# A Chebyshev graph convolution block on one core: the dense work of a block two groups later, its aggregate placed ready transposed, node numbers written to PSUM, the first own rows loaded whole, unread products ahead of the look-ups

## The chip, the cores and the metric

The kernel runs on one core of a Trainium2 chip. Its engines are TensorE (PE; PEld is its weight load), VectorE (DVE), ScalarE (ACT), GpSimd (POOL) and SyncE (SP), which here only issues DMAs. The metric is the device time in microseconds (us); the time before is 2028.2 us, the median of three runs (2027.43 to 2034.34).

## The reference

`x` has N = 6250 rows of D = 512 floats; `src` and `dst` have E = 100000 entries, sorted by `dst`. Cut to what matters:

```python
h = maximum(layernorm(x), 0)
deg = segment_sum(ones(E), src);  dinv = where(deg > 0, 1 / sqrt(max(deg, 1)), 0)
norm = -dinv[src] * dinv[dst]
conv = lambda h, W0, W1, b: h @ W0 + segment_sum(h[src] * norm[:, None], dst) @ W1 + b
h = layer_norm(conv(h, W1_0, W1_1, b1)) * gamma + beta
h = where(h >= 0, h, 0.01 * h)
out = x + conv(h, W2_0, W2_1, b2)
```

So each of the two layers gathers 100000 rows of 2 KB by index, adds them into 6250 nodes, and multiplies the nodes' own rows and the sums by a 512x512 matrix each. All is 32-bit floating point.

## The kernel before

**First phase** (before `usual_path`). x is read in tiles of 128 nodes, and its mean and variance are taken. The degrees are counted by one-hot matmuls in bf16 (lines 417 and 440). The table of the first layer, `tab[0]`, gets 528 numbers a row: 512 of relu(layernorm(x)) times dinv (L340) and dinv itself (L478). Meanwhile POOL already gathers the first 76 chunks of 128 edges out of raw `x` (L291); their normalization is made up for later.

**Chunks, units, groups, blocks.** The edges are cut into 782 chunks of 128. One indirect DMA (L548), issued by POOL, fetches the 128 rows of a chunk into a slot of a ring in SBUF (`places`; the first twelve chunks sit in tiles that later hold weights and biases, `lent`). Three chunks are a unit, which adds into 32 columns of nodes; four units are a group of 12 chunks and 128 columns. Group 0 has only one unit, and there are 66 groups in a layer, so group g holds the chunks from 12g - 9 to 12g + 2. A block is 128 nodes; there are 49, and a block's nodes lie in two or three groups.

**Work of a group.** `choose` on DVE writes the numbers of the nodes that a column stands for (`node`, L678, 128x128) and compares them with the edges' destinations to a 0/1 matrix `sel` (L689, 128x384). In layer 0, for chunks from 76 on, `scale` (L729) multiplies `sel` by the dinv that came with each gathered row. `sums` (L745) then multiplies the 12 gathered chunks by `sel` on PE, with 12 matmuls of 128x512 into `ps`, and ACT copies the sums to SBUF (`agg`, L760). The first 76 chunks hold raw x: for them PE looks up scale and shift of each edge by matmuls (`look_up` L598 with L601, L604 and L607 on DVE, `find` L583 and L586), and ACT applies them in place (L609, a Relu per chunk).

**Work of a block.** `place` (L781) adds the rows of the block's two or three groups into `an_ps` by 0/1 matrices `there` (L768, DVE); ACT scales the result by -dinv (L880); PE turns it (four transposes, L888) and DVE copies that to `aT` (L890). The node's own rows `h` come back from the table by eight DMAs (`load_h`, L622: 32 rows apart in a fashion that lets DVE's 32x32 transposes, L632, finish the turn). PE multiplies both: own rows by one matrix (L648, four matmuls of 128x512), aggregate by the other (L643, four more, into the same PSUM sum). `finish` adds the bias, normalizes and writes the row to the second layer's table (L849 to L866), or adds x and writes the output (L843 to L846). The last four blocks' own rows are done ahead (`early`).

**What sets the order.** The order of PE, POOL and SP is written out by hand in `usual_path`: what the program says is the order of the queue. DVE's and ACT's order is the scheduler's, which is held by `issue_after` at some places. In the order before, block work of a group's end comes around that group's `sums`: for groups 3 to 5 of layer 0 behind them, else ahead of them, and the second product (L643) one step later (`left`).

**The ring.** `ring` (L46) says which chunk sits in which slot and which chunk had it before, and `gather_to` lets POOL issue only those gathers whose slot was read by a `sums` that has already been written down. POOL's queue is in order, so a gather whose slot is not yet read holds all later ones. Before, the ring has 55 slots, and from a hundred or so chunks on it shrinks slowly, lap by lap: to 35 in the first layer and to 26 in the second.

Of the kernel before, what the change touches and what calls it, by code (L numbers as in the profile page):

```python
# [26 lines left out]
Q = 32  # L27
NQ = P // Q
STEP = 3
DRIFT = 32  # L30
RE = 14
# [8 lines left out]
NARROW = 26  # L40

# [6 lines left out]
def ring(chunks, lent, most, full):  # L48
# [25 lines left out]
def gnn_kernel(  # L74
# [54 lines left out]
    def dup(ap, n):  # L129
# [16 lines left out]
    ndeg = const.tile([P, NB], F32, name="ndeg")  # L146
# [31 lines left out]
    nodes_ps = stay.enter_context(tc.tile_pool(name="nodes_ps", bufs=1, space=bass.MemoryType.PSUM)).tile(  # L178
        [P, D], F32, name="nodes_ps")
    assert NQ * NS + 1 <= D - P  # L180
# [169 lines left out]
    def turn_dst(wps):  # L350
# [17 lines left out]
        first_ps = nodes_ps[:, : NQ * NS + 1]  # L368
# [78 lines left out]
    with tc.tile_pool(name="fold", bufs=1) as dp, tc.tile_pool(  # L447
# [15 lines left out]
        nc.vector.tensor_mul(ndeg, ndinv, dinv)  # L463

    for i0, n in others:
# [9 lines left out]
        nc.vector.tensor_copy(places[:, RE + i0 : RE + i0 + n, D : D + 1], dinv[:, cols, None])  # L475
        make_table(i0, n)
    early = NB - LAST
# [13 lines left out]
def usual_path(tc, have):  # L491
    nc = tc.nc
    (x, out, tab, root, ndeg, ndinv, sidx, dlx, iota_r, w_sb, W2_1, W2_0, w_late, ident, eps, ones, first, nodes_ps, node_of, minus,
     unsorted, dinv, sdinv, bias1, bias2, gam, bet, unseen, unit, N, E, D, NB, NC, NU, NS, KD, rows, places, R,
     load_rest, sc, pick, quads, src_hi, zero_row, p_id, lent, X, src, W) = (
        have[n] for n in ("x out tab root ndeg ndinv sidx dlx iota_r w_sb W2_1 W2_0 w_late ident eps ones first nodes_ps node_of "
                          "minus unsorted dinv sdinv bias1 bias2 gam bet unseen unit N E D NB NC NU NS KD rows places "
                          "R load_rest sc pick quads src_hi zero_row p_id lent X src W").split())
    AHEAD = 2
    SOON = range(3, 6)  # L500
# [10 lines left out]
    with ExitStack() as es:  # L511
# [12 lines left out]
        own_row, begun = {}, set()  # L524
# [9 lines left out]
        slots, prev = ring(NC, X, R + LATER, R)  # L534
# [54 lines left out]
        def look_up(tag):  # L589
# [7 lines left out]
            for j in range(4):  # L597
# [5 lines left out]
            both = pool.tile([P, D], F32, name="an")[:, : 8 * NB].rearrange("p (j k b) -> p j k b", j=4, k=2)  # L603
            nc.vector.tensor_tensor(both, at_lo[:, :, : 2 * NB].rearrange("p j (k b) -> p j k b", k=2),  # L604
                                    is_hi[:, :, None, :].to_broadcast([P, 4, 2, NB]), op=OP.mult)
# [19 lines left out]
        def load(layer, i):  # L625
            if i not in EARLY:
                load_h(layer, i, pool.tile([P, D], F32, name="h", bufs=AHEAD))
# [819 lines left out]
```

## Time and profile before

| | us |
|---|---|
| median of three runs | 2028.2 |
| the profiled execution | 2038.83 |
| its span | 2037.0 |
| PE busy | 1637.0 (80%) |
| DVE busy | 745.5 (37%) |
| ACT busy | 332.8 (16%) |
| POOL busy | 1494.5 (73%) |
| gathers of L548 out of the tables (`sidx` 1191, `lidx` 270) | 1134.0 + 256.1 |

The profile page names an engine's busy time, then groups of equal instructions: line, engine, operation, output<-input, shape, count, then busy time, mean duration of one in ns, idle time just ahead of them and who ended it. The windows view gives, for each stretch of the span, each engine's busy time with the number of its instructions in brackets, then TensorE's granted clock, the share of the DMA engines and GB/s. The timeline has a row for each instruction or run of equal ones: start, duration, engine, line, operation, tiles, count, and in brackets how long the engine had waited and for whom. A busy engine is not the same as the bound: PE is busy 80% of the span, and POOL 73%, but POOL's time has an issue gap behind each gather.

### The profile page before, as it was taken

Reading aid. Unit: us, or ns where it says so; the run is one execution under the profiler, and the core shown is the slowest. Engines: PE = TensorE matmul, PEld = TensorE weight load, DVE = VectorE, ACT = ScalarE, POOL = GpSimd, SP = SyncE. Lnnn points to the kernel's source line nnn. Section 1 sums busy time; section 2 is a strip of 40 time slices with the busy share of each in tenths; the row PEclk is TensorE's granted clock in tenths of the full one; section 3 lists DMA queues with packets and bytes.
Section 4 is the critical chain, followed back from the end, with each engine's and each line's share of the span. In section 5 each row is a group of like instructions: output and inputs, shape, how many; then the busy total and the mean of one; then the engine's idle time right before and its main releaser. Section 6 shows DMA issues by size and latency. Waiting matters only on the chain.

```text
span 2037.0 us, 18838 instructions
## 1 busy us (share of the span) xinstructions
PE 1637.0 (80%) x6458; PEld 626.0 (31%) x6458; DVE 745.5 (37%) x1554; ACT 332.8 (16%) x605; POOL 1494.5 (73%) x1578
## 2 busy tenths in 40 slices
PE   5478997678787677878888887888888878888888
PEld 4443342223232222333233222223222222223333
DVE  8965554243453333543453221222222222222221
ACT  8775111011110110111110000000000000000000
POOL 4576677777777777777777777777777777777775
PEclk9779998889888889888899899999998899989999
DMA  9998788888888888888887888888888888888885
GB/s 340 392 328 250 231 249 241 243 237 247 253 255 243 237 242 241 251 245 253 248 235 234 254 249 252 241 256 245 246 253 249 244 253 255 237 254 261 261 245 174
DMA packets 225518, 515.56 MB, mean 253 GB/s; under 512 B 38796, under 2 KB 90570, under 8 KB 225414
## 3 DMA queue, kind: packets, MB, share of 16 engines
q0 software_dynamic: 125120, 415.88, 68.7%
q1 hardware_dynamic: 100253, 98.38, 15.1%
q8 instruction: 53, 0.87, 0.2%
q14 instruction: 52, 0.42, 0.1%
q10 hardware_dynamic: 40, 0.02, 0.0%
HBM read 475.25 MB, written 38.86 MB: 252 GB/s over the span
## 4 chain that ended last, share of the span: by engine, by line
POOL 42%; PE 18%; issue 18%; DMA 14%; DVE 7%; ACT 1%; SPq 0%; DVEq 0%; POOLq 0%; ACTq 0%
POOL places L548 42%; DMA places<-tab,sidx 9%; PE ps L745 5%; PE u_ps L643 4%; PE u_ps L648 4%; DMA places<-tab,lidx 3%; PE an_ps L781 2%; DVE hi L417 1%; DVE lo L417 1%; DMA w<-in_L_gnn_W_dram 1%; DVE st L852 1%; PE hT_ps L888 1%; DVE u_ps L849 1%; PE hT_ps L598 1%; DMA h<-tab 1%
## 5 line engine op out<-in xcount | busy, mean ns | idle before, releaser
L548 POOL DMA_INDIRECT places<-tab,sidx x1191 | 1134.0, 952 | 378.0 <-issue 336.1
L745 PE MATMUL ps<-places,sel 128*32 128x512 f32 x3104 | 522.0, 667 | 169.2 <-DMA places<-tab,sidx 96.2
L781 PE MATMUL an_ps<-agg,there 128*128 128x512 f32 (+1 forms) x554 | 277.0, 634 | 109.4 <-ACT agg L760 109.4
L548 POOL DMA_INDIRECT places<-tab,lidx x270 | 256.1, 948 | 82.3 <-issue 78.1
L745 PEld LDWEIGHTS ps<-places,sel 128*32 128x32 f32 x3104 | 102.3, 117 | 555.5 <-DMA places<-tab,sidx 205.1
L689 DVE TENSOR_TENSOR sel<-dlx,nodes_ps 128x384 f32<-128x384 f32 (+3 forms) x134 | 72.4, 541 | 445.5 <-PE ps L745 432.9
L648 PE MATMUL u_ps<-w,hT 128*128 128x512 f32 x392 | 182.0, 608 | 25.4 <-DVE hT L632 22.5
L781 PEld LDWEIGHTS an_ps<-agg,there 128*128 128x128 f32 (+1 forms) x554 | 108.1, 201 | 263.6 <-issue 141.7
L760 ACT ACTIVATE agg<-ps 128x512 f32<-128x512 f32 (+2 forms) x130 | 76.2, 588 | 639.8 <-PE ps L745 612.2
L648 PE MATMUL u_ps<-places,hT 128*128 128x512 f32 x392 | 177.8, 597 | 0.0
L643 PE MATMUL u_ps<-w,aT 128*128 128x512 f32 x384 | 173.3, 594 | 2.3 <-DVE aT L890 2.3
L643 PE MATMUL u_ps<-places,aT 128*128 128x512 f32 x384 | 173.4, 593 | 0.8 <-DVE aT L890 0.8
L729 DVE TENSOR_TENSOR sel<-sel,places 128x384 f32<-128x384 f32 (+9 forms) x76 | 35.3, 466 | 368.6 <-DMA places<-tab,sidx 363.9
L855 ACT ACTIVATE sd<-mv,eps 128x1 f32<-128x1 f32 (+1 forms) x49 | 14.4, 295 | 600.4 <-DVE mv L853 600.3
L632 DVE STREAM_TRANSPOSE hT<-h 128x512 f32<-128x512 f32 x90 | 63.6, 707 | 129.0 <-PE u_ps L648 120.6
L648 PEld LDWEIGHTS u_ps<-w,hT 128*128 128x128 f32 x392 | 72.7, 196 | 102.5 <-issue 76.5
L643 PEld LDWEIGHTS u_ps<-w,aT 128*128 128x128 f32 x384 | 72.4, 190 | 94.4 <-issue 89.9
L643 PEld LDWEIGHTS u_ps<-places,aT 128*128 128x128 f32 x384 | 72.6, 190 | 92.2 <-issue 90.3
L768 DVE TENSOR_SCALAR there<-iota_r,node_of 128x128 f32<-128x128 f32 (+1 forms) x286 | 67.2, 299 | 76.3 <-PE an_ps L781 76.3
L648 PEld LDWEIGHTS u_ps<-places,hT 128*128 128x128 f32 x392 | 71.4, 192 | 73.8 <-issue 73.8
L291 POOL DMA_INDIRECT places<-in_x_dram,sidx x63 | 59.9, 951 | 40.0 <-DVE hi L417 11.8
L880 ACT ACTIVATE an<-an_ps,ndeg 128x512 f32<-128x512 f32 x45 | 30.9, 688 | 329.5 <-PE an_ps L781 329.5
(196 smaller groups left out, 1160.8 us busy)
## 6 DMA issues: line engine op xcount, KB each, us to landing
h<-tab SPq DMA_DIRECT2D x360, 64.0 KB
places<-tab,sidx POOLq DMA_INDIRECT x1191
xt<-in_x_dram SPq DMA_DIRECT2D x48, 256.0 KB
out_dram<-t SPq DMA_DIRECT2D x48, 256.0 KB
tab<-t SPq DMA_DIRECT2D x46, 256.0 KB
tab<-places SPq DMA_DIRECT2D x22, 528.0 KB
places<-in_x_dram SPq DMA_DIRECT2D x5, 1792.0 KB
places<-tab,lidx POOLq DMA_INDIRECT x270
```

The source lines that it names most:

```text
L291: got = nc.gpsimd.indirect_dma_start(out=lent[t] if t < X else places[:, t - X, :D], out_offset=None, in_=x, in_offset=bass.IndirectOffset ...
L417: made = nc.vector.tensor_tensor(t, s[:, g * 2 * GJ : (g + 1) * 2 * GJ].rearrange("p (j s) -> p j s", s=2)[:, :, None, :] .to_broadcast([E ...
L548: nc.gpsimd.indirect_dma_start(out=places[:, slot(t), :] if own_scale else zr(layer, t), out_offset=None, in_=x if layer == 0 and t < RAW ...
L632: nc.vector.transpose(hT.rearrange("p k (a i) -> p k a i", i=Q), own_h.pop(i).rearrange("p (a k d) -> p k a d", a=NQ, d=Q))
L643: nc.tensor.matmul(u_ps[:r], hT[:, kc, :r], w[:, kc, :], start=(start and kc == 0), stop=(stop and kc == KD - 1))
L648: nc.tensor.matmul(u_ps, hT[:, kc, :], w[:, kc, :], start=(kc == 0), stop=(stop and kc == KD - 1))
L689: nc.vector.tensor_tensor(sel[:, q : q + k, :w, :], of, node[:, q : q + k, None, :].to_broadcast([P, k, w, Q]), op=OP.is_equal)
L729: last = nc.vector.tensor_tensor(v, v, places[:, k : k + hi - lo, D : D + 1].to_broadcast([P, hi - lo, Q]), op=OP.mult)
L745: members.append(nc.tensor.matmul(to, sel[:, q, s, :], rows_of, start=(s == 0), stop=(s == len(chunk[q]) - 1 and (cnt is None or chunk[q][ ...
L760: nc.scalar.activation(agg[g][: n * Q, lo : lo + w], ps[: n * Q, lo : lo + w], AF.Copy)
L768: behind[1] = nc.vector.tensor_scalar(t[:m, :r], iota_r[:m, :r], node_of[:m, g : g + 1], -(1.0 + i * P), op0=OP.subtract, op1=OP.is_equal)
L781: all_of.append(nc.tensor.matmul(placed[i][:r], t[:m, :r], agg[g][:m, :], start=(g == inside[i][0]), stop=(g == inside[i][-1])))
```

## The change

1. **Order of the block's work.** From group 0 of layer 0 and group 4 of layer 1 on, up to group 49, a group's `sums` go first. Behind them come both products of a block that was placed two groups earlier, and then `place` of a block that is now complete (`far_left`, `FAR`). From group 46 (`CLOSER`) the distance is one group, from group 50 (`NEAR`) the order is the near one as before. `scale` of the next group and `choose` of the one after are asked for ahead of a group's sums. Every second block uses a second set of `hT` and `there` tiles, which lie in two slots of the ring.
2. **Place.** The aggregate is the stationary operand and `there` the moving one, so the block's aggregate comes out turned: four columns of D times two or three groups, matmuls of 128x128 into `hT_ps`. ACT's scaling (L880) and PE's transposes (L888) fall away. The factor -dinv is applied in `finish`, and the own rows' part gets a PSUM tile of its own, from which DVE adds bias (or x) into the tile of own rows (L690).
3. **The ring** has 53 slots until 159 chunks before a layer's end, and then loses eight a lap.
4. **Node numbers**: `node` is written to PSUM from `first` in SBUF; before, `first` lay in PSUM too.
5. **First own rows whole**: blocks 0 and 1 of layer 0 get their own rows by one DMA each, and PE turns them by 16 matmuls.
6. **Unread products**: twice seven 128x512 matmuls that nobody reads, ahead of the first look-ups (`WARM`).
7. Smaller: three tiles for own rows, loaded once; the look-up's product is formed in place in PSUM; at the layer's end nothing stands between the two halves of a block.

On PE, in layer 0, from the sums of group 6 to those of group 7 (`ps` is a group's sums, `an_ps` the placed aggregate, `u_ps` the products, `w_83` and `w_84` the matrices). Before:

```order
L745 MATMUL ps<-places,sel 32x512 x12
L888 MATMUL hT_ps<-ident,an 128x128 x4
L648 MATMUL u_ps<-w_84,hT 128x512 x4
L643 MATMUL u_ps<-w_83,aT 128x512 x4
L781 MATMUL an_ps<-agg,there 128x512
L781 MATMUL an_ps<-pre,there 128x512
L781 MATMUL an_ps<-agg,there 128x512
L745 MATMUL ps<-places,sel 32x512 x12
```

The third block's products and the next block's place stand between the two groups' sums. Now, from the sums of group 6 on (its names: L655 the turn of own rows that were loaded whole, L687 and L669 the two products, L805 place):

```order
L767 MATMUL ps<-places,sel 32x512 x12
L655 MATMUL hT_ps<-ident,h 32x128 x16
L687 MATMUL an_ps<-w_83,hT 128x512 x4
L669 MATMUL u_ps<-w_82,aT 128x512 x4
L767 MATMUL ps<-places,sel 32x512 x12
L655 MATMUL hT_ps<-ident,h 32x128 x16
L687 MATMUL an_ps<-w_83,hT 128x512 x4
L669 MATMUL u_ps<-w_82,aT 128x512 x4
L805 MATMUL hT_ps<-there,pre 128x128
```

Here stand the products of block 0, which in the order before came behind the sums of groups 3 and 4; block 1 follows behind group 7.

On SP at the start of `usual_path` (`h` own rows, `w_83` and `w_84` the layer's matrices). Before:

```order
L478 DMA tab_60<-dinv 128x31x1
L622 DMA h<-tab_60 32x4x128 x8
L244 DMA w_83<-in_L_gnn_W_1_dram 128x4x512
L70 DMA w_84<-in_L_gnn_W_0_dram 32x4x512 x4
L249 DMA bias_78<-in_L_gnn_b_dram 128x512
```

And now:

```order
L486 DMA tab_60<-dinv 128x31x1
L629 DMA h<-tab_60 128x512 x2
L246 DMA w_82<-in_L_gnn_W_1_dram 128x4x512
L74 DMA w_83<-in_L_gnn_W_0_dram 32x4x512 x4
L251 DMA bias_77<-in_L_gnn_b_dram 128x512
```

Both blocks' own rows are two DMAs of 128x512 ahead of the matrices, where eight of 32x4x128 for each block stood (the second block's behind the biases).

On DVE, between the look-ups of the raw chunks (`src_hi`, `an`, `ac`). Before:

```order
L601 TENSOR_TENSOR t<-src_hi,iota_r 128x196
L689 TENSOR_TENSOR sel<-dlx,nodes_ps 128x384
L632 STREAM_TRANSPOSE hT<-h 128x512
L678 TENSOR_TENSOR nodes_ps<-nodes_ps,iota_r 128x128
L689 TENSOR_TENSOR sel<-dlx,nodes_ps 128x384
L678 TENSOR_TENSOR nodes_ps<-nodes_ps,iota_r 128x128
L604 TENSOR_TENSOR an<-hT_ps,t 128x392
```

And now (L700 the node numbers, L711 `sel`, L809 the copy of the turned aggregate, L792 `there`, L615 the look-up's product):

```order
L612 TENSOR_TENSOR t<-src_hi,iota_r 128x196
L700 TENSOR_TENSOR node_ps<-first,iota_r 128x128
L711 TENSOR_TENSOR sel<-dlx,node_ps 128x384
L700 TENSOR_TENSOR node_ps<-first,iota_r 128x128
L809 COPY aT<-hT_ps 128x512
L792 TENSOR_SCALAR there<-iota_r,node_of 128x128
L615 TENSOR_TENSOR hT_ps<-hT_ps,t 128x4x98
```

The transpose of own rows no longer stands ahead of the look-up's product, and L700 reads two SBUF tiles where L678 read one.

The diff, cut to its core:

```diff
@@ ring
-        if size == most:
-            size = full
-        elif len(slots) > most + 2 * full:
-            size -= 2 if size > WIDE else 3 if size > NARROW and len(slots) > chunks + full else 0
+        layer, at = divmod(len(slots), chunks)
+        size = full if chunks - at > 3 * full else max(NARROW if layer else WIDE, size - DROP)
@@ end of the first phase
     for i0, n in others:
...
+        if i0 != others[-1][0]:
+            nc.tensor.matmul(busy[:, :n], ident, rs_all[:, cols], start=True, stop=True)
+            for _ in range(WARM):
+                nc.tensor.matmul(busy, ident, dlx[:, 1 : 1 + D], start=True, stop=True)
         make_table(i0, n)
@@ usual_path
-        slots, prev = ring(NC, X, R + LATER, R)
+        slots, prev = ring(NC, X, R + LATER, R - 2)
+        odd_hT = places[:, R - 1, :D].rearrange("p (k i) -> p k i", k=KD)
+        odd_there = places[:, R - 2, :D].rearrange("p (k i) -> p k i", k=KD)
@@ look_up
-            both = pool.tile([P, D], F32, name="an")[:, : 8 * NB].rearrange("p (j k b) -> p j k b", j=4, k=2)
+            both = at_lo[:, :, : 2 * NB].rearrange("p j (k b) -> p j k b", k=2)
@@ load_h, own
+        def whole(layer, i):
+            return layer == 0 and i < AHEAD
...
+            if whole(layer, i):
+                nc.sync.dma_start(to, of[i * P : (i + 1) * P, :D])
+                return
...
+            if whole(layer, i):
+                ps = psum.tile([P, KD, P], F32, name="hT_ps")
+                for kc in range(KD):
+                    for a in range(NQ):
+                        nc.tensor.matmul(ps[a * Q : (a + 1) * Q, kc, :], of[:, kc, a], ident, start=True, stop=True)
+                turned = nc.vector.tensor_copy(hT, ps)
@@ choose
-            nc.vector.tensor_tensor(node[:, :n, :], nodes_ps[:, at : at + n, None].to_broadcast([P, n, Q]),
+            nc.vector.tensor_tensor(node[:, :n, :], first[:, at : at + n, None].to_broadcast([P, n, Q]),
                                     iota_r[:, None, :Q].to_broadcast([P, n, Q]), op=OP.add)
@@ place
-                all_of.append(nc.tensor.matmul(placed[i][:r], t[:m, :r], agg[g][:m, :], start=(g == inside[i][0]),
-                                               stop=(g == inside[i][-1])))
+            for kc in range(KD):
+                for t, g in zip(there, some):
+                    m = Q * (unit[g + 1] - unit[g])
+                    all_of.append(nc.tensor.matmul(ps[:, kc, :r], agg[g][:m, kc * P : (kc + 1) * P], t[:m, :r],
+                                                   start=(g == some[0]), stop=(g == some[-1])))
...
+            aT = pool.tile([P, KD, P], F32, name="aT")
+            behind[2] = nc.vector.tensor_copy(aT[:, :, :r], ps[:, :, :r])
@@ finish
-                nc.vector.tensor_add(v, v, pre.pop(i)[:r] if i in EARLY else bias1[:r])
+                nc.vector.scalar_tensor_tensor(v, v, ndinv[:r, i : i + 1], pre.pop(i)[:r], op0=OP.mult, op1=OP.add)
@@ the loop over groups
+                far = FAR[layer] <= g < NS - NEAR
...
+                if far:
+                    back = 2 if g < NS - CLOSER else 1
...
                     sums(layer, g, sel, chunk, cnt)
...
+                    if far:
+                        with ExitStack() as order:
+                            for ins in prepared:
+                                order.enter_context(tc.issue_after(ins.ins))
+                            for k, _, aT, hT in [one for one in far_left if one[1] <= g - back]:
+                                if layer == 1 and k not in own_x:
+                                    load_x(k)
+                                dense(layer, k, hT or own(layer, k), aT)
+                            far_left = [one for one in far_left if one[1] > g - back]
+                            while inside[i].stop <= g + 1 - back:
+                                far_left.append([i, g, place(layer, i, inside[i]), None])
+                                i += 1
```

More of the change, by code (lines that the diff above doesn't have):

```diff
@@ L644, in products @@
                                  stop=(stop and kc == KD - 1))
-        def own_products(u_ps, hT, w, stop):
-            for kc in range(KD):
-                nc.tensor.matmul(u_ps, hT[:, kc, :], w[:, kc, :], start=(kc == 0), stop=(stop and kc == KD - 1))
         def load_early(layer, i):
@@ L1013, in usual_path @@
                             order.enter_context(tc.issue_after(ins.ins))
-                        scaled = scale(sel, chunk)
+                        done.add(k)
+                        return scale(*some)
+                if layer == 0 and g not in done:
+                    scaled = scale_for(g, (sel, chunk))
                 with ExitStack() as order:
@@ L1072, in usual_path @@
                     if g == at:
-                        early(layer, k)
+                        own_part(layer, k, own(layer, k), "u_ps", 2)
                 if g == NS - 2:
```

192 lines of the change are left out of this document (103 added, 89 removed).

## Prediction

> **What bounds the kernel now.** I read the page's groups and chain first, then windows of 50 us, then what POOL waited for, and last the timeline where a window stands out. The page, the group of the table gathers and the chain by engine:
>
> ```profile
> POOL 42%; PE 18%; issue 18%; DMA 14%; DVE 7%; ACT 1%; SPq 0%; DVEq 0%; POOLq 0%; ACTq 0%
> L548 POOL DMA_INDIRECT places<-tab,sidx x1191 | 1134.0, 952 | 378.0 <-issue 336.1
> ```
>
> POOL and "issue" are 60% of the chain, and both belong to one thing: a gather holds POOL for 0.95 us, and the next starts 0.30 us behind it. The windows (PE, PEld, DVE, ACT, POOL, granted clock, DMA share, GB/s) show the rate:
>
> ```profile
> 150.00:200.00 50.00, 41.40 (x177) 19.64 (x179) 26.47 (x59) 24.72 (x38) 32.59 (x35) 0.93 0.84 249
> 200.00:250.00 50.00, 50.00 (x210) 19.75 (x207) 25.10 (x54) 9.85 (x17) 33.22 (x35) 1.00 0.78 230
> 250.00:300.00 50.00, 50.00 (x217) 19.58 (x216) 28.79 (x63) 9.59 (x17) 37.82 (x40) 1.00 0.87 250
> 1450.00:1500.00 50.00, 39.69 (x152) 12.76 (x145) 10.96 (x23) 3.77 (x6) 37.80 (x41) 0.97 0.83 254
> ```
>
> From 250 us on there are 40 or 41 gathers in 50 us, one each 1.25 us, early and late alike, whether PE is busy all of the time or 79% of it. So POOL's issue of gathers is the bound, and PE, though busy 80% of the whole span, follows. A group of 12 gathers takes 12 x 1.2525 = 15.03 us. The two windows before hold 35 each: five or more gathers are missing in both. What POOL waited for:
>
> ```profile
> POOL places L548 <- issue: 414.4, 1357, 0.9
> POOL places L548 <- PE ps L745: 10.4, 15, 5.4
> POOL places L548 <- ACT pre L760: 6.7, 1, 6.7
> ```
>
> The timeline shows both places:
>
> ```profile
> 183.45 0.96 POOL L548 DMA_INDIRECT places<-tab,sidx  x1 [0.30 <-issue]
> 184.99 4.48 PE L745 MATMUL ps<-places,sel 128*32 128x512 f32 x24
> 189.80 0.94 POOL L548 DMA_INDIRECT places<-tab,sidx  x1 [5.39 <-PE ps L745]
> ...
> 208.59 0.95 POOL L548 DMA_INDIRECT places<-tab,sidx  x1 [0.30 <-issue]
> 212.59 2.78 PE L745 MATMUL ps<-places,sel 128*32 128x512 f32 x24
> 216.23 0.95 POOL L548 DMA_INDIRECT places<-tab,sidx  x1 [6.69 <-ACT pre L760]
> ```
>
> Between 183.45 and 189.80 lie 6.35 us, 5.10 more than a period; between 208.59 and 216.23 7.64, 6.39 more. The first window lacks five gathers, 6.3 us, of which 5.1 are this gap, so that with smaller waits about 13 us are lost; I take 13.1 (ten gathers missing in the two windows are 12.5). By the ring the first held gather is chunk 114, in the slot that group 5 frees, and the second chunk 130 = 75 + 55, which waits for group 7; each starts when that group's sums end (189.47, 215.37). So PE is late there, and this is the only loss beyond 132 us that the change touches in full.
>
> **Why PE is late.**
>
> ```profile
> 115.98 1.13 PE L598 MATMUL hT_ps<-sc,xt 128*128 128x98 f32 x8 [0.34 <-DVE an L604]
> 105.92 5.75 ACT L609 ACTIVATE w<-w,ac 128x512 f32<-128x512 f32 x8
> ...
> 117.09 8.57 ACT L609 ACTIVATE places<-places,ac 128x512 f32<-128x512 f32 x12 [1.97 <-DVE ac L607]
> 126.04 8.56 ACT L609 ACTIVATE places<-places,ac 128x512 f32<-128x512 f32 x12
> 138.38 0.71 DVE L632 STREAM_TRANSPOSE hT<-h 128x512 f32<-128x512 f32 x1 [8.46 <-DMA h<-tab]
> 140.80 2.03 PE L598 MATMUL hT_ps<-sc,xt 128*128 128x98 f32 x8 [9.52 <-DVE an L604]
> 158.24 5.25 PE L648 MATMUL u_ps<-w,hT 128*128 128x512 f32 x8 [2.90 <-DMA w<-in_L_gnn_W_dram]
> 215.80 3.60 PE L648 MATMUL u_ps<-w,hT 128*128 128x512 f32 x8
> ```
>
> DVE stands 8.46 us at block 0's transpose until its own rows have come, and the look-up's product queued behind it holds PE for 9.52. The look-ups then run cold (2.03 for 1.13), PE waits 2.90 for the matrix, and the product behind that takes 5.25 for 3.60. These are 9.52 + 2.90 + 1.65 = 14.1 us, about the 13.1 that POOL then loses.
>
> **The change, part by part.**
>
> *Order and first own rows: -13.1 us.* The transposes of blocks 0 and 1 leave DVE, and their products go behind the sums of groups 6 and 7. What paces the look-ups then is ACT: 8.56 us for 12 chunks. At 134.6 it has scaled 36 chunks (the first twelve in four tiles from 105.92 on, of which the row of eight is shown). Group 5 ends with chunk 62, 27 more: 19.3 us, with three copies of sums of 0.6 and 2.8 for its sums about 159. Group 6 needs 12 more and is through at about 169. Then block 0: a turn in 16 matmuls (32 records, 4.2 by the price of place below) and two products of 3.60 (one shape), so group 7's sums end at about 184; block 1 and a place later group 8 at about 201. Due are, in a row of gathers without stalls (chunk 114 at 183.45 + 1.25 = 184.7, 1.2525 each): group 5 at 184.7, group 7, whose first slot is now wanted by chunk 75 + 53 = 128, at 202.2, group 8 by chunk 140 at 217.3. The tightest is some 16 us early, so two slots fewer (2.5 us) do no harm. If the matrix is still late, by the 2.90 above, that too is covered. The least gain is none (the backlog of block work meets the stall at a later group), the most 13.1; I take 13.1, since the two tightest groups have 16 us and more.
>
> *Place: 0.* Before, a block costs 2.74 (place) and 0.66 (transposes):
>
> ```profile
> 215.30 0.66 PE L888 MATMUL hT_ps<-ident,an 128*128 128x128 f32 x4
> 305.17 2.74 PE L781 MATMUL an_ps<-agg,there 128*128 128x512 f32 x6
> 2025.23 1.04 PE L805 MATMUL an_ps<-end_there,agg 128*128 128x106 f32 x8
> ```
>
> Now it is 12 matmuls of 128x128, 24 records (each matmul has two). By the last row, the nearest in shape, a record takes 0.13, so 24 take 3.1, against 3.40. With 49 blocks to 66 groups, 0.74 blocks a group, PE works 2.78 + 0.74 x (3.6 + 3.6 + 3.1) = 10.4 us a group, under 15.03, and 13.1 where a block falls into it. Its cover is POOL's period: it goes at 0.40 us a record. That ACT's 0.69 for the scaling falls away and DVE adds the own part (0.3 to 0.8, a 128x512 operation) is hidden by the same: DVE is busy 10.96 of 50 us in the late window.
>
> *Node numbers: +1.5 us.* The operation now reads two SBUF tiles, and DVE operations that do so lengthen a gather that starts within them:
>
> ```profile
> 257.75 0.55 DVE L729 TENSOR_TENSOR sel<-sel,places 128x384 f32<-128x384 f32 x1
> 257.79 1.33 POOL L548 DMA_INDIRECT places<-tab,sidx  x1 [0.30 <-issue]
> 1546.23 0.30 DVE L678 TENSOR_TENSOR nodes_ps<-nodes_ps,iota_r 128x128 f32<-128x128 f32 x1
> 1546.23 0.95 POOL L548 DMA_INDIRECT places<-tab,sidx  x1 [0.30 <-issue]
> ```
>
> The first pair has two SBUF inputs, and the gather grew from 0.95 to 1.33: what was left of DVE's operation (0.51), less 0.13. In the second, the old node operation with one input in PSUM, nothing grew, although both began together. An operation of 0.30 can lengthen a gather by at most 0.30 - 0.13 = 0.17. Of 130 such operations a gather begins inside some 0.30 / 1.2525 = 24%, 31 in all, and where in the operation it begins is even: the mean is 0.17 x 0.17 / 2 / 0.30 = 0.05, and the sum 1.5. The ends are 0 (the lengthening is absent when the output is PSUM) and 130 x 0.17 = 22 (DVE always set free by the very event that starts a gather). The Trainium skill, "SBUF — State Buffer", section "Who interferes with whom", speaks against this edit: a VectorE instruction with two SBUF inputs contends with a GpSimd instruction that reads SBUF, and by its summary the second fully blocks until the first is done. By the full 0.30 for each of the 31 that would be up to 9 us; the trace shows 0.38 of 0.51, in the same sense but not in full.
>
> *Ring: 0.* Besides the early groups, the distance matters only if PE lags by more than the slots of a group allow; in layer 1 the new ring is wider nearly to the end, so that nothing is lost there.
>
> *Unread products: 0.* The first look-up waits and then runs cold:
>
> ```profile
> 101.97 2.00 PE L598 MATMUL u_ps<-sc,xt 128*128 128x98 f32 x8 [13.23 <-DMA tab<-places]
> ```
>
> PE is idle for 13.23 us. Fourteen products of 128x512 take 12.6 by the row of 3.60 for four, and 18.4 by that of 5.25; so they end between 0.6 ahead of the first look-up and 5.2 behind it, and I take 2.6 behind. Three look-ups then take 1.13 for 2.00, which gives that back. ACT, not PE, paces what follows. Ends: -1 and +5, with the reserve of 16 us behind them.
>
> *SP's queue: 0.* Own rows come by two DMAs, ahead of the matrices as before; from then on loads of h stand a group or two ahead of their use, 15 to 30 us, and a load that stands behind a store waits only for that store's `finish`. POOL's queue is not passed by anything.
>
> *Tail: -0.6 us.*
>
> ```profile
> 1995.24 1.04 PE L745 MATMUL ps<-places,sel 128*32 128x512 f32 x2 [1.36 <-DMA places<-tab,lidx]
> 2018.77 0.95 POOL L548 DMA_INDIRECT places<-tab,lidx  x1 [0.30 <-issue]
> 2021.57 2.77 PE L745 MATMUL ps<-places,sel 128*32 128x512 f32 x12
> ```
>
> The last gather starts at 2018.77; gathers of this kind land about 3.7 us later, at 2022.5, inside the last sums. PE runs through from 1995.24, so the tail is bound by both within a microsecond: ends 0 and -1.2.
>
> Sum: -13.1 + 1.5 - 0.6 = -12.2. The profiled execution took 2038.83 and would take 2026.6. The median of the runs, 2028.2, is 10.6 below it, so that the forecast is 2028.2 - 12.2 = 2016.0. (What can be told from no change is 0.5%, 10 us: below 2018 it is faster.) In runs that are 10.6 shorter the stall may be smaller too; that is the forecast's weak side.
>
> **The rivals.** *The stall is only moved or smaller*: the products of blocks 0 to 3 all come between groups 6 and 10, where PE is already full (50.00 of 50 us from 200 to 300), or ACT's scaling waits elsewhere. For it: PE has no idle time to make up in up to 300 us. Against: the 16 us of reserve. With half of 13.1 left, 2022; with all of it, 2029. Nearly all within 0.5%.
>
> *The change doesn't do what it says*: own rows and matrix come late for another reason (many DMAs in flight: DMA share is 0.84 there), and group 5 stays late. Then 2028.2 + 1.5 - 0.6 = 2029.
>
> *Slower, by the lock of SBUF*: each node operation costs POOL more than 0.17 because DVE's next one (L689) is chained to it. It ends slower by 0.5% once the 130 operations cost (13.1 + 0.6 + 10) / 130 = 0.18 us each if the stall goes, or 0.08 if it stays; at 0.30 each they cost 39, and 2028.2 - 13.7 + 39 is 2053. Against: only some of the operations meet a gather's start. The page "SBUF — State Buffer" of the Trainium skill is this rival's rule, told above.
>
> *Slower, PE becomes the bound*: a place record at 0.45 us instead of 0.13 gives 2.78 + 0.74 x (7.2 + 10.8) = 16.1 a group, 1.1 more than the period, over 110 groups about 120 us; it decides from 0.40. The nearest row says 0.13 and nothing says 0.4.
>
> **How the numbers follow.** The forecast 0.53; the moved stall 0.27; not doing what it says 0.06; the lock 0.09; PE as the bound 0.05. Faster are the forecast's cases (0.53), within 0.5% the moved stall and the unchanged one (0.33), slower the last two (0.14). The range reaches down to 2008, the forecast with the node operation at nothing (-1.5), the tail at -1.2, and some 5 us for waits that no row here assigns; up to 2032, past the case in which the stall stays in full and the first look-ups come late: 0.14 is left out above, little below. The forecast's own range is 2010 to 2018.
>
> **What would show it.** Right: in the profile after, 40 gathers in each of the windows from 150 to 250 us; POOL's waits for the sums together under 3 us; no wait of DVE for own rows near 130 us; place records near 0.13 us; a few tens of gathers of 1.0 to 1.1 us beside L700. Wrong: 5 us gaps between gathers at another place before 400 us, or a mean gather of L548 above 0.96 us.

## The result and the profile after

The kernel after took 2024.51 us (median of 20 runs, 2020.89 to 2028.53) against 2031.12 for the kernel before (20 runs): a ratio of 0.9967, with a 95% interval of 0.9960 to 0.9974, so 6.6 us less, where 12.2 were forecast. By the bound of 0.5% that is no change. The profiled execution took 2025.95 us (span 2024.2), 12.9 less than that of before: nearly the forecast. So the two profiles show the forecast, and the runs half of it.

On the page of the kernel after, the groups of the table gathers and of place (L559 was L548, L805 was L781):

```profile
L559 POOL DMA_INDIRECT places<-tab,sidx x1191 | 1131.8, 950 | 366.7 <-issue 337.6
L805 PE MATMUL hT_ps<-there,agg 128*128 128x128 f32 (+1 forms) x1008 | 153.1, 278 | 2.1 <-ACT agg L782 1.9
```

The gathers' idle time is 11.3 us less than before (378.0). The windows of after, with the same columns as before:

```profile
150.00:200.00 50.00, 44.56 (x292) 24.21 (x285) 22.52 (x53) 18.16 (x28) 37.78 (x40) 0.93 0.85 258
200.00:250.00 50.00, 46.71 (x259) 23.21 (x258) 27.97 (x61) 6.49 (x12) 37.97 (x40) 0.97 0.88 246
250.00:300.00 50.00, 35.00 (x155) 15.72 (x155) 18.91 (x43) 3.53 (x7) 37.88 (x40) 0.83 0.85 238
1450.00:1500.00 50.00, 40.93 (x198) 17.91 (x200) 13.02 (x27) 1.79 (x3) 37.82 (x41) 0.92 0.85 253
```

POOL starts 40 gathers in both early windows, where it started 35. What POOL waited for in after:

```profile
POOL places L559 <- issue: 414.9, 1362, 0.3
POOL places L559 <- ACT places L619: 7.8, 13, 3.2
POOL places L559 <- PE ps L767: 4.6, 15, 0.3
```

No wait for sums is longer than an issue gap of 0.3 (before, 5.4 and 6.7), so the 4.6 in all are 15 ordinary gaps, although the prediction's sign was under 3; the 3.2 stands ahead of the first gather out of the table, where before waits too (1.9). On PE's timeline of after, the sums of groups 5, 7 and 8, and one place:

```profile
163.17 4.95 PE L767 MATMUL ps<-places,sel 128*32 128x512 f32 x24
186.07 2.78 PE L767 MATMUL ps<-places,sel 128*32 128x512 f32 x24
200.39 2.78 PE L767 MATMUL ps<-places,sel 128*32 128x512 f32 x24
...
1985.83 2.84 PE L805 MATMUL hT_ps<-there,agg 128*128 128x128 f32 x24
```

They end at 168, 189 and 203, where the forecast had 159, 184 and 201; all are in time, with 13 us or more in hand. Place takes 0.12 us a record. The look-ups of these groups go slower than ACT's scaling would allow, which the forecast took for their pace. ACT waits 1.5 us and then 5.5 us for them:

```profile
159.21 8.57 ACT L619 ACTIVATE places<-places,ac 128x512 f32<-128x512 f32 x12 [5.54 <-DVE ac L617]
```

In the first half of the longer wait PE works on block 0's place (152.3 to 156.6 us), which stands between the look-ups.

To compare profiles below, one number is used: the time from the start of gather 113 to that of gather 160, less 47 periods of 1.2525. This **early loss** is 11.7 us in the profile of before and 0.4 in that of after. The **tail** is the time from the start of the last gather to the end of the span: 18.3 and 19.4.

### The profile page after: what moved, and what is told of

The parts are those of the page before. It is cut to its first block, busy times and chain, and to the rows that moved or that the text cites. A ratio compares the mean times of both kernels' runs of the same rounds, so it can differ in the third digit from the quotient of the medians.

```text
span 2024.2 us, 21750 instructions
## 1 busy us (share of the span) xinstructions
PE 1637.7 (81%) x7886; PEld 766.8 (38%) x7886; DVE 798.2 (39%) x1641; ACT 266.3 (13%) x509; POOL 1492.3 (74%) x1578
## 5 line engine op out<-in xcount | busy, mean ns | idle before, releaser
L559 POOL DMA_INDIRECT places<-tab,sidx x1191 | 1131.8, 950 | 366.7 <-issue 337.6
L559 POOL DMA_INDIRECT places<-tab,lidx x270 | 255.6, 947 | 82.3 <-issue 77.4
L711 DVE TENSOR_TENSOR sel<-dlx,node_ps 128x384 f32<-128x384 f32 (+3 forms) x134 | 72.0, 539 | 407.6 <-PE ps L767 397.0
L687 PE MATMUL an_ps<-w,hT 128*128 128x512 f32 x248 | 129.4, 670 | 68.1 <-DVE h L690 43.4
L669 PE MATMUL u_ps<-w,aT 128*128 128x512 f32 x384 | 176.0, 602 | 7.4 <-DVE t L886 6.5
L669 PE MATMUL u_ps<-places,aT 128*128 128x512 f32 x384 | 173.3, 593 | 0.0
L805 PE MATMUL hT_ps<-there,agg 128*128 128x128 f32 (+1 forms) x1008 | 153.1, 278 | 2.1 <-ACT agg L782 1.9
L805 PEld LDWEIGHTS hT_ps<-there,agg 128*128 128x128 f32 (+1 forms) x1008 | 132.9, 192 | 28.0 <-issue 21.4
L687 PE MATMUL an_ps<-places,hT 128*128 128x512 f32 x240 | 115.5, 625 | 1.6 <-DVE hT L658 1.6
L669 PEld LDWEIGHTS u_ps<-w,aT 128*128 128x128 f32 x384 | 73.6, 193 | 102.2 <-issue 92.1
L669 PEld LDWEIGHTS u_ps<-places,aT 128*128 128x128 f32 x384 | 72.6, 190 | 92.0 <-issue 92.0
L687 PEld LDWEIGHTS an_ps<-w,hT 128*128 128x128 f32 x248 | 50.2, 213 | 147.1 <-issue 64.4
L687 PE MATMUL an_ps<-w,places 128*128 128x512 f32 x112 | 61.6, 701 | 52.2 <-DVE h L690 52.2
L809 DVE COPY aT<-hT_ps 128x512 f32<-128x512 f32 x96 | 65.7, 684 | 89.4 <-PE hT_ps L805 89.3
L805 PE MATMUL hT_ps<-there,pre 128*128 128x128 f32 x584 | 100.1, 276 | 0.0
L805 PEld LDWEIGHTS hT_ps<-there,pre 128*128 128x128 f32 x584 | 84.3, 192 | 15.1 <-issue 14.7
```

Of the source, the lines that this page charges most:

```text
L559: nc.gpsimd.indirect_dma_start(out=places[:, slot(t), :] if own_scale else zr(layer, t), out_offset=None, in_=x if layer == 0 and t < RAW ...
L669: nc.tensor.matmul(u_ps[:r], hT[:, kc, :r], w[:, kc, :], start=(start and kc == 0), stop=(stop and kc == KD - 1))
L687: nc.tensor.matmul(u_ps, hT[:, kc, :], (w_late[:, 1] if layer else w_sb[1])[:, kc, :], start=(kc == 0), stop=(kc == KD - 1))
L711: behind[3] = nc.vector.tensor_tensor(sel[:, q : q + k, :w, :], of, node[:, q : q + k, None, :].to_broadcast([P, k, w, Q]), op=OP.is_equal)
L805: all_of.append(nc.tensor.matmul(ps[:, kc, :r], agg[g][:m, kc * P : (kc + 1) * P], t[:m, :r], start=(g == some[0]), stop=(g == some[-1])))
L809: behind[2] = nc.vector.tensor_copy(aT[:, :, :r], ps[:, :, :r])
```

## The experiments

**Two more profiles.** The kernels before and after once more, without an edit.

> The kernel before once more, unchanged, for a second profiled execution. The profiled execution of before took 2038.83 us and lost 5.1 us ahead of the gather at 189.80 and 6.4 ahead of that at 216.23; the kernel after loses neither, and its profile is 12.8 us shorter, but its 20 runs are only 6.6 us below those of before. Theory A (the early stall is all of the gain, and its size varies from execution to execution, so that the profiled one of before was a bad one): the two gaps come to between 4 and 10 us here, and the span follows them. Theory B (the stall is some 13 us in every execution, and something in the change gives about 6 us back in most runs): the two gaps come to 11 to 13 us again.

> The kernel after once more, unchanged: a second profile, and its time on the same chip as the three that follow. Theory A (the early stall is gone in every execution): no gap over 1 us between the gathers from 150 to 230 us, and about 2 us more between the last VectorE instruction and the end of the program than before has (before 5.4 and 6.0 us in two profiles, after 7.7). Against before on a chip like the first two: 0.996 to 0.998.

Before once more had an early loss of 9.1 us, with a span of 2033.0; windows and waits of this second profile:

```profile
150.00:200.00 50.00, 44.03 (x192) 20.03 (x192) 26.74 (x59) 25.76 (x38) 36.06 (x39) 0.94 0.89 271
200.00:250.00 50.00, 50.00 (x198) 20.51 (x198) 26.05 (x56) 7.91 (x14) 31.93 (x34) 0.99 0.77 219
```

```profile
POOL places L548 <- ACT pre L760: 8.3, 1, 8.3
POOL places L548 <- PE ps L745: 5.4, 15, 1.1
```

The wait for group 5 is down to 1.1 us, that for group 7 is 8.3. Together they are 9.4, near the upper end of theory A's 4 to 10. So the stall differs between executions of the same kernel, as theory A has it; but this execution, 2034.93 us, was the slowest of its 12, and no median one was profiled. Its time against before itself was 1.0004 (0.9994 to 1.0014). After once more was 0.9971 of before (0.9959 to 0.9982), with an early loss of 0.7 and a tail of 20.4.

**Before without the loads of the first own rows.** Zeros stand in their place, so this kernel leaves their share of the result out.

```diff
@@ load_h of the kernel before
+            if layer == 0 and i < AHEAD:
+                nc.vector.memset(to, 0.0)
+                return
```

> Before, with the own rows of blocks 0 and 1 of layer 0 set to zero instead of loaded from the table (their 16 DMAs and their share of the result are left out; all else is as before). This takes DVE's wait of 8.46 us for these rows away, and nothing else of the change is made. Theory A (the wait of DVE for own rows is what makes the early groups late, and the stall is all that the change won): the gap ahead of the first gather held for group 5 is under 1 us and that for group 7 under 4, and the time falls by 4 to 7 us, most of the 6.6 that the whole change won. Theory B (the stall is 13 us in all runs): it falls by 9 to 12. Theory C (the gain comes from the order of the later groups or from the end): it falls by less than 2.

It was 0.9977 of before (0.9967 to 0.9988), 4.7 us less. Its windows, and its longest wait for the sums:

```profile
150.00:200.00 50.00, 45.27 (x193) 20.61 (x193) 26.63 (x57) 25.02 (x37) 37.90 (x40) 0.97 0.89 264
200.00:250.00 50.00, 50.00 (x216) 19.55 (x215) 28.61 (x64) 9.58 (x17) 36.58 (x39) 1.00 0.86 248
```

```profile
POOL places L548 <- ACT pre L763: 2.1, 1, 2.1
```

The early loss is 1.9 us. But the edit takes away more than VectorE's wait. Without the 16 loads ahead of it, the matrix comes in time too, and PE's first product waits for nothing (before, 2.90 us) and takes 3.60 instead of 5.25:

```profile
149.39 3.60 PE L651 MATMUL u_ps<-w,hT 128*128 128x512 f32 x8
```

So the loading of the first own rows, by VectorE's wait and by the late matrix behind it, is the cause of most of the stall in before; what each of the two does alone was not measured. To take the loads away gives some 70% of what the whole change gives.

**Only the first groups, and none.** The order far apart only up to group 11 of layer 0 (with blocks still open closed at the switch), and nowhere:

```diff
-                far = FAR[layer] <= g < NS - NEAR
+                far = layer == 0 and g < 12
...
-                if g == NS - NEAR:
+                if not far and far_left:
```

> After, with sums first and blocks two groups later only up to group 11 of layer 0; from group 12 on and in layer 1 the near order, as before. Theory A (only the first ten groups matter): within 2 us of after, 5 to 8 us below before, and 40 gathers in each 50 us from 150 us on. Theory C (the order of the later groups gives a part of the gain): 3 us or more slower than after.

It was 0.9964 of before (0.9950 to 0.9978): with the near order in all but the first twelve groups nothing is lost. The far order of the later groups is worth nothing here.

```diff
-FAR = (0, 4)
+FAR = (99, 99)
```

> After, with the near order throughout (blocks' work ahead of the sums but in groups 3 to 5 of layer 0); place by turned products, whole first rows, the ring and the unread products stay. Theory A (for the stall it is the order of the first groups that counts): PE's turn of block 0's rows, which now stands between the look-ups, waits for these rows, and gaps of 4 us or more come back from 170 to 230 us; 3 to 8 us slower than after. Theory D (the whole loads are what counts): within 1.5 us of after.

It was 1.0047 of before (1.0030 to 1.0063), 15 us slower than after on the same chip. Its windows and waits:

```profile
150.00:200.00 50.00, 42.25 (x269) 23.59 (x268) 27.84 (x59) 23.38 (x34) 35.14 (x37) 0.90 0.85 259
200.00:250.00 50.00, 45.85 (x227) 22.21 (x226) 25.26 (x53) 5.91 (x11) 27.97 (x30) 1.00 0.67 192
```

```profile
POOL places L559 <- ACT pre L782: 12.7, 1, 12.7
POOL places L559 <- PE ps L767: 10.3, 16, 2.5
```

The early loss is 16.9 us, more than in before. But not for the reason expected: PE's turns of the rows of block 0 (at 151) and block 1 (at 172) did not wait for these rows, but stood behind look-ups. On PE's timeline of this kernel:

```profile
151.15 1.08 PE L655 MATMUL hT_ps<-ident,h 128*32 128x128 f32 x32 [1.00 <-DVE xt L597]
171.94 1.56 PE L655 MATMUL hT_ps<-ident,h 128*32 128x128 f32 x32 [1.69 <-DVE xt L597]
178.80 4.66 PE L767 MATMUL ps<-places,sel 128*32 128x512 f32 x24
183.39 3.70 PE L687 MATMUL an_ps<-w,hT 128*128 128x512 f32 x8
```

Group 5's sums end at 183.5, 15 us later than in after, with turn, products and places of blocks ahead of them. So the loading of own rows and the place of the block work are two ways to the same stall; after needs the far order in the first dozen groups. Why its near order does worse than that of before (16.9 against 1.9 without the loads of own rows) was not taken apart; its turns, places and smaller ring are all in it.

**How the first own rows come, and the end of the program.**

```diff
         def whole(layer, i):
-            return layer == 0 and i < AHEAD
+            return False
```

> After, with the own rows of blocks 0 and 1 loaded by 16 DMAs and turned by VectorE, as before; on the chip where its twin ran, every kernel was 16% slower or more, so that it told nothing of this. Theory A (what counts is that VectorE's transposes stand behind the look-ups, not how the rows come): within 1.5 us of after, no gap over 1 us between the gathers from 150 to 230 us. Theory D (the whole loads are needed): VectorE waits some 8 us for own rows again and a gap of 4 us or more comes back.

It was 0.9953 of before (0.9935 to 0.9972), and the early loss 0.0. VectorE's transpose of block 0's rows, behind the look-ups, waits for nothing:

```profile
175.59 0.70 DVE L658 STREAM_TRANSPOSE hT<-h 128x512 f32<-128x512 f32 x1
```

So the whole loads are not needed. This kernel's tail is 18.0 us, that of the other kernels made from after 18.9 to 20.4. The difference lies behind the last VectorE instruction. This instruction, in before and in after:

```profile
2030.63 0.42 DVE L827 TENSOR_TENSOR t<-u_ps,pre 106x256 f32<-106x256 f32 x1 [1.30 <-PE u_ps L643]
```

```profile
2016.08 0.42 DVE L854 TENSOR_TENSOR t<-u_ps,pre 106x256 f32<-106x256 f32 x1 [1.30 <-PE u_ps L669]
```

From its end to the end of the span are 6.0 us in before and 7.7 in after (5.4 and 8.6 in the second profiles). In the windows of the last 12 to 25 us, what SyncE waited for (the line of its last waits) and the packets of one instruction queue, in before:

```profile
SPq L486 <- SPq L486: 3.2, 1, 3.2
```

```profile
q14 instruction: 6, 0.05, 1.1%
```

and in after:

```profile
SPq L494 <- SPq L494: 5.0, 2, 2.9
```

```profile
q14 instruction: 7, 0.06, 0.7%
```

In after SyncE halts twice between its last waits, and a seventh packet of 8 KB of instructions comes in. (The second halt lies from 4.2 to 2.2 us before the end, and the packets at 3.8 and 2.9 fall into it; that SyncE waits for them is read from this alone.) To tell the instructions from the way the rows are loaded, each whole load was cut into eight:

```diff
-                nc.sync.dma_start(to, of[i * P : (i + 1) * P, :D])
+                for lo in range(0, P, 16):
+                    nc.sync.dma_start(to[lo : lo + 16], of[i * P + lo : i * P + lo + 16, :D])
```

> After, with each of the two whole own-row loads cut into eight DMAs of 16 rows: 14 more SyncE instructions at the start, nothing else. In five profiles of after and its relatives the end of the program comes 7.4 to 8.6 us behind the last VectorE instruction, with a seventh packet of instructions in the last 6 us, and in before and the kernel with 14 more SyncE instructions 5.4 to 6.3 us, with six. Theory A (SyncE's instructions are fetched in blocks, and in after a block's border falls between its last waits): the seventh packet is gone here, and the tail from the last gather to the end is 17.4 to 18.3 us instead of 19.3 to 20.4; the time is 1 to 2.5 us below after. Theory H (the old way of loading own rows did it): the tail stays at 19 to 20 us.

In its profile:

```profile
SPq L494 <- SPq L494: 3.6, 1, 3.6
```

```profile
q14 instruction: 6, 0.05, 1.0%
```

The second halt and the seventh packet are gone, and from the last VectorE instruction to the end are 6.3 us. Of the 17 profiles of kernels made from after, the five with 14 more loads show six packets behind the last VectorE instruction and 5.4 to 6.3 us from there to the end, the twelve others seven packets and 7.4 to 8.6 us. (Before shows six, with its first 16 loads and without them.) The cut loads are still whole rows that PE turns, so it is the number of SyncE's instructions, as theory A has it, and not the old way of loading. This run's time tells nothing of 2 us, for a reason that has a part of its own below.

**The node operation.**

```diff
             nc.vector.tensor_tensor(node[:, :n, :], first[:, at : at + n, None].to_broadcast([P, n, Q]),
                                     iota_r[:, None, :Q].to_broadcast([P, n, Q]), op=OP.add)
+            for _ in range(16 if layer == 1 else 0):
+                nc.vector.tensor_tensor(node[:, :n, :], first[:, at : at + n, None].to_broadcast([P, n, Q]),
+                                        iota_r[:, None, :Q].to_broadcast([P, n, Q]), op=OP.add)
```

> After, with the node operation of each group of layer 1 done 17 times instead of once (the same numbers are written again): 1040 more VectorE operations of 0.3 us with two SBUF inputs, on an engine that is busy 12 of 50 us there. It measures the disputed price by itself. In the profile of after 26 gathers began inside a node operation and were longer by 0.026 us on average, 0.7 us in all for 130 operations. Theory A (that is the price): 1040 operations cost 5 to 6 us. Theory B (the operation costs about 2.8 us for 130, the difference that the kernel with node numbers read from PSUM showed): some 22 us. Theory C (a gather is held for the whole rest of the operation, 0.15 us on average, at 24% of the operations): 37 us.

> The same 1040 additional node operations, but with the node numbers read from PSUM (one SBUF input), as before. All theories that speak of two SBUF inputs expect 0 to 1 us more than the kernel that reads them from PSUM once, so 2020 to 2022 us, and gathers of 0.95 us beside them. If it is longer by as much as its sister, it is not the SBUF input that counts, but VectorE's work itself.

In layer 1, the groups of gathers and of the additional operation with two SBUF inputs:

```profile
L559 POOL DMA_INDIRECT places<-tab,sidx x584 | 558.3, 956 | 356.6 <-issue 163.2 <-PE ps L770 123.1 <-remote 39.3
L559 POOL DMA_INDIRECT places<-tab,lidx x211 | 200.9, 952 | 126.8 <-issue 70.2 <-PE ps L770 34.3 <-remote 18.4
...
L703 DVE TENSOR_TENSOR node_ps<-first,iota_r 128x128 f32<-128x128 f32 x967 | 289.3, 299 | 27.5
```

and with one input in PSUM:

```profile
L559 POOL DMA_INDIRECT places<-tab,sidx x589 | 560.2, 951 | 355.0 <-issue 163.3 <-PE ps L770 118.3 <-remote 27.5
L559 POOL DMA_INDIRECT places<-tab,lidx x211 | 200.0, 948 | 128.0 <-issue 68.7 <-PE ps L770 28.0 <-remote 26.6
...
L703 DVE TENSOR_TENSOR node_ps<-node_ps,iota_r 128x128 f32<-128x128 f32 x967 | 287.8, 298 | 25.8
```

A gather is 4 to 5 ns longer on average beside the first. Some 217 gathers began inside one of the additional operations with two SBUF inputs; summed over those that are over 20 ns longer than 0.946 us it is 4.9 us (4.4 when the kernel ran once more), against under 0.1 with one input in PSUM. So 1000 operations with two SBUF inputs cost POOL 4 to 5 us, and the 130 of the change 0.5 to 0.6. The rule of the Trainium skill, "SBUF — State Buffer", section "Who interferes with whom", that such an instruction contends with a GpSimd instruction that reads SBUF, shows in the difference between the two kernels; that the second would wait for the whole rest of the first from the gather's start on, 0.155 us on average or 34 us in all, does not. (A gather that reads SBUF only some time after its start would fit both; the traces don't show when it does.)

The times of these two kernels, 1.0806 and 1.0728 of before, were taken on a chip where PE is the bound (below). They differ by 18 us, near theory B. But the pair with the operation once a group differs about as much on another such chip (1.0754, with the cut loads, and 1.0686), so the difference does not grow with the number of node operations, and the same kernel's runs scatter by over 30 us. They can't decide about the price of one operation.

With the node numbers read from PSUM once a group, as in before:

```diff
-        first_ps = wps.tile([P, NQ * NS + 1], F32, name="first_ps")
+        first_ps = node_ps[:, : NQ * NS + 1]
...
-            node = node_ps[:, : NQ * Q].rearrange("p (q e) -> p q e", q=NQ)
-            nc.vector.tensor_tensor(node[:, :n, :], first[:, at : at + n, None].to_broadcast([P, n, Q]),
+            node = node_ps[:, D - P :].rearrange("p (q e) -> p q e", q=NQ)
+            nc.vector.tensor_tensor(node[:, :n, :], node_ps[:, at : at + n, None].to_broadcast([P, n, Q]),
```

> After, with the node numbers read from PSUM as before, all else as after. Theory A (the node operation with two SBUF inputs costs POOL 0 to 2 us in all): 0 to 2 us faster than after, so 6 to 9 us below before, and no gather beside a node operation is longer than 0.96 us. Theory B (it is the node operation that gives back some 6 us in most runs): 5 to 7 us faster than after, about 13 below before.

> After, with one tile moved: the product that gives the first node of each unit (first_ps) is made in the node tile's unused columns, as before, and not in a tile of the first phase's PSUM pool; the node operation reads `first` from SBUF, as in after. The kernel that read the node numbers from PSUM was some 2.8 us faster than after, and in its profile 4.6 of 5.2 us lay in the first 112 gathers, where no node operation differs much. Theory F (the tile in the first phase's pool costs it, by a wait for a free buffer): this one is 2 to 4 us faster than after too. Theory B (the SBUF input of the node operation costs it): it is as fast as after. Theory G (chance of 6 runs): both within 1 us of after.

The first was 0.9953 of before (0.9940 to 0.9965, 6 runs), 2.8 us better than after. But in its profile the first 112 gathers account for 4.6 of the 5.2 us by which its span is below that of after, and beside node operations there is under 1.7 to gain. The second, with only the first node's tile moved, was 0.9970 (0.9957 to 0.9983), as after. So neither the tile nor the gathers' lengthening explains the 3 us; chance of six runs, on another chip than after's, is possible. It stays open.

**The unread products.** Without the two times seven products (`WARM` loop taken out):

> After, without the two times seven unread products (the short ones of line 480 stay). Theory A (ACT's scaling, not PE, sets the pace of the first groups, and they have over 10 us in hand): the first look-ups take 2.0 us again for 1.13, and the time is within 1.5 us of after. Theory E (the products give a part of the gain): 2 us or more slower than after.

The first look-ups took 2.00 us, as expected, where after's take 1.10. What that costs isn't known: its time, too, is one of the following.

**Chips on which PE is the bound.** On three chips before itself took 2360 to 2385 us. There, all kernels made from after were slower than before: cut loads 1.0754 (1.0725 to 1.0783), without unread products 1.0727 (1.0705 to 1.0748), rows not whole 1.0678, node numbers from PSUM 1.0686 and 1.0573, 17 node operations 1.0806 and 1.0779 (from PSUM 1.0728), and node numbers from PSUM with 16 loads 1.0702 and 1.0534. After itself was not run there; the cut loads differ from it only by 14 DMAs. The kernel of the last pair joins the two edits that gave time back:

> After, with node numbers read from PSUM and the first own rows loaded by 16 DMAs. By theory B and the shorter end (2 us): 0.9935 to 0.995 of before. By theory G and the shorter end: 0.9955 to 0.9965. In its profile six packets of instructions in the last 6 us, and 5.4 to 6.3 us from the last VectorE instruction to the end.

It was not run on a chip of the usual speed, so whether the two gains add up isn't known. The chain by engine, from the page of the kernel with cut loads, and the longest of what PE waited for:

```profile
PE 56%; issue 19%; another core or an unknown queue 9%; POOL 8%; DVE 4%; DMA 2%; ACT 1%; SPq 0%; DVEq 0%; ACTq 0%; POOLq 0%
```

```profile
PE ps L768 <- issue: 310.6, 254, 17.2
PE hT_ps L806 <- issue: 150.5, 151, 6.2
```

and the same wait of PE in after on the first chip:

```profile
PE ps L767 <- issue: 38.9, 21, 3.5
```

On that chip PE starts 651 of its matmuls and weight loads just 0.70 or 1.40 us (within 0.014) after the one before, 599 us together; in after on the first chip 8 do. 471 of them belong to sums, 142 to place. The granted clock in the runs of before is 0.84 to 0.85 there and 0.90 to 0.92 on the others; in the kernels made from after it is 0.81 to 0.82 there and 0.90 to 0.93 on the others. After has 15772 matmuls and weight loads where before has 12916. That they are why it loses more, and is granted less, on such a chip fits, but was not tried; nor do the traces say what slows PE there. No profile of before was taken on these chips, so that PE is its bound there too is not shown.

## Why the prediction was half right

- *POOL's issue is the bound, a gather each 1.25 us.* Right, in every profile on chips of the usual speed.
- *The stall goes, for the reason named.* Right: 35 gathers became 40 in both windows, and without the loads of own rows before loses most of its stall (1.9 us left). The prediction's three terms (9.52, 2.90 and 1.65) went together there.
- *Its size, -13.1 us: the step that failed first.* It was read from one execution of 2038.83 us, while before's other runs lie between 2026 and 2037. The prediction named this weakness (a profiled execution 10.6 us above the median) and yet carried the 13.1 over to the median in full. Even that execution lost 11.7 by the early loss, its two gaps 11.5, so that 13.1 was read too high by 1.4; the second profile lost 9.1. The stall of a median execution was not seen. Two estimates of it are 6.6 us (the kernel without the loads ran 4.7 faster, and its profile still lost 1.9) and 8.9 (6.6 won by the whole change, plus 1.7 at the end, plus 0.6 for the node operation).
- *The pace of the first groups* was taken from ACT's scaling alone. The look-ups also wait for PE and VectorE, and group 5 ended 9 us later than forecast; the reserve, forecast as 16 us at the least, was still 13 and covered it.
- *Tail, -0.6: wrong in sign.* From the last gather to the end of the last sums it went from 5.6 to 5.0, just as forecast; but then SyncE's second halt adds 1.7, and the tail grows by 1.1 (by 3.0 between the second profiles).
- *Node numbers, +1.5.* The mechanism is right, the size is 0.5 to 0.6: a gather that began inside such an operation was lengthened by 0.02 us on average, not by 0.05. The rival by which it decides (0.18 us for each operation) did not come; they cost 0.005. An open 3 us of one kernel stand beside it.
- *Place, 0.* Right on the first chip: 2.84 us for 24 records, PE busy 1637.7 us in all (1637.0 before). ACT's and VectorE's shares were hidden as forecast.
- *First own rows whole* was part of the -13.1. They are not needed for it, and by 14 fewer loads on SyncE they bring the longer end.
- *Ring, SP's queue: 0.* No run speaks against it, and none took them alone. *Unread products: 0*: open; the first look-up starts 1.6 us later with them (103.57 for 101.97), where 2.6 were forecast, and takes 1.10 for 2.00.
- *The rival "the stall is only moved or smaller"* named 2022 us, closer to the measured time than the forecast, but not by its mechanism: in after nothing of the stall is left and none has moved; there was less of it in before.
- *The rival "PE becomes the bound"*, put at 0.05 for a place record of 0.45 us, did not happen by that price, but on three chips PE is the bound of the kernels made from after, and they lose 5 to 8%.

## What to carry to other kernels

A stall that one profile shows is worth its mean over executions, not its size in that one: where the profiled execution lies far above the median of the runs, its stalls are the first to be marked down, and a second profile tells by how much. An order that puts the work others wait for first needs to be kept only as far as the stall reaches; here the first dozen groups. And where PE has little in hand, more and smaller matmuls at the same busy time may be a risk on chips that hold PE back; here this fits, and was not tried by itself.

## What was not expected of the hardware

- A load of instructions can fall between the last waits of SyncE: with one more packet of 8 KB the end comes about 2 us later (7.4 to 8.6 us for 5.4 to 6.3), and 14 DMAs more or fewer at the start of the program decide it.
- The same kernel took 2030 us on some chips and 2360 on others, 16% more, and the sign of this change differs with them: -0.3% on the first, +7.5% (with cut loads) on one of the others. Whether it is the chip itself, or what else went on there at the time, isn't known.
